# One weighted product of a two-layer graph kernel goes over to Strassen's scheme on pairs of row tiles

## The chip, the cores and the metric

The kernel runs on one NeuronCore of a Trainium2 chip. The metric is the device time of one execution in microseconds (us). Before the change it is 2158.61 us, the median of three runs (2158.42 to 2158.98).

The engines have the names of the profile: PE is TensorE (matmuls), PEld its loading of the stationary operand, DVE is VectorE, ACT is ScalarE, POOL is GpSimd, SP is SyncE, which mostly issues DMAs. Each engine has a queue of its own and works through it in order.

## The reference, cut to what matters

There are 3327 rows of 512 numbers (padded to 3328, that is 26 row tiles of 128), and an adjacency matrix of 3327 x 3327. Everything is float32.

```python
# layer 0
h = maximum(layernorm(x), 0)
q, k, v = h @ Wq.T + bq, h @ Wk.T + bk, h @ Wv.T + bv
a = q @ k.T / sqrt(512) + adj + adj
x = x + softmax(a) @ v
# layer 1
h = maximum(layernorm(x), 0)
A2 = adj + eye
d = diagonal(A2) ** -0.5
temp = A2 @ h @ W.T
x = x + relu((d[:, None] * A2 * d[None, :]) @ temp)
```

The kernel multiplies the unscaled exponentials P with h first and with Wv afterwards: `softmax(a) @ v` is `(P @ h @ Wv.T) / rowsum + bv`, because the rows of the softmax sum to one. So layer 0 ends, for each row tile, with a product of 128 x 512 by 512 x 512, a scaling by 1 / rowsum (`rs`), and the addition of `bv` and `x`. Layer 1 has a product of the same shape with W, scaled by `sd`, the d above.

## The kernel before, in words

**Scores.** 52 steps (four groups of columns, 13 pairs of row tiles) compute the scores. The function `fetch(k + 2)` loads the adjacency for two steps ahead on SP's queue. The queues of DVE, PE, POOL and SP are held to the order in which the code was written (`in_order`).

**The three large products.** Then come three products with a matrix of 3328 x 3328: g = 0 is P with h of layer 0, g = 1 is A2 with h of layer 1, g = 2 is A2 with `temp`. Each is cut by Strassen's scheme at the outside into seven parts (`ORDER`: p5, p1, p6, p7, p2, p3, p4), each part into two strips of columns (s = 0, 896 wide, and s = 1, 768 wide), each strip into seven steps: six with seven matmuls (t = 0 to 5) and an odd one with four (t = None). That makes 294 steps. The matmuls are 448 or 384 columns wide, half a strip. `Step.sums` makes three sums on DVE for each step, two steps ahead (`four_sums`, L164 to L166); `Right.make` makes the right sides (L171 to L174, L878 to L884); `Gather.first` (L962 to L966) and `Gather.rest` (L982) take the results of a strip out of PSUM at its end: `first` after the step t = 5, `rest` after the odd step. `Gather.seed` (L956, on ACT) puts a start value into the banks of the next strip.

**What is done beside the steps.** `run(k)` writes step k: its loads, its matmuls, with products of other work `inserted` between them, and then the DVE work that waits its turn in the list `waiting`. The dictionary `between` says what else belongs to step k; `number_of(g, r, s, t)` gives the number of a step. `post` puts a store off to the next step, on ACT's queue.

* Jobs: 52 sums (`Job`, L1017, 896 or 768 wide, on DVE) that layer 1 needs, one about every three steps from step 7 to step 164.
* The product with Wv: from step 79 (g = 0, p3, s = 1, t = 2) on, one row tile a step, 26 in all. `attend_load` loads x two steps ahead on ACT's queue; `attend` runs four matmuls of 512 columns into one PSUM bank after the step's matmuls (L1026), then on DVE the scaling with x added (L1038), `bv` added (L1039), and `norm` (L185 to L189 on DVE, L191 on POOL). `attended`, one step later, makes the row of h for layer 1 on ACT (L1045) and stores it. Wv and a copy of `bv` for all partitions are loaded at step 2 (`prepare`).
* The product with W (`Temp`): from step 177 on, one pair of row tiles for two steps. This one is already by Strassen's scheme: the 256 x 512 of the pair are four blocks of 128 x 256, and seven products of two 256-wide matmuls each stand for the eight block products. The two halves of one bank take the products in turn. After each product the bank's half is added into the result, which is called settling here: by ACT for p2, p5, p6 and p4 (L1091, a scaled write), by DVE for m1, p3 and p7 (L1093). Eight sums of 128 x 128 on DVE (L1077) make the left sides. The products stand at fixed places among the matmuls of steps k and k + 1, in this order:

```python
PARTS = (("p2", 1, True, 0, 1), ("m1", 0, True, 0, -1), ("p5", 1, False, 3, -1), ("p6", 0, False, 1, -1),
         ("p3", 1, False, 1, 1), ("p7", 0, False, 3, 1), ("p4", 0, False, 2, 1))
AFTER = ((0, 0), (0, 2), (0, 4), (0, 6), (1, 1), (1, 3), (1, 5))
```

The second column of `PARTS` is the half of the bank, the third says whether it starts anew, the fourth is the quarter of the result. `AFTER` says for each product the step (0 for k, 1 for k + 1) and after how many matmuls of it the product comes. The matmuls of a product that accumulates must wait until the settling before has read the same half.

## Time and profile before

The profiled execution took 2159.13 us; its span, which the views show, is 2157.3 us.

| | busy, us | share of the span |
|---|---|---|
| PE | 2137.5 | 99% |
| DVE | 1652.0 | 77% |
| PEld | 1180.9 | 55% |
| ACT | 273.1 | 13% |
| POOL | 68.1 | 3% |

| work on the profile's page | line | busy, us | mean of one, ns |
|---|---|---|---|
| matmuls of the product with Wv, 512 columns, from `ct` | L1026 | 61.6 | 592 |
| the same, from `part` | L1026 | 32.9 | 592 |
| matmuls of the product with W, 256 columns, from `rows` | L1087 | 53.5 | 380 |
| scaling and x (20 of the 26) | L1038 | 15.0 | 749 |
| adding `bv` (20 of the 26) | L1039 | 13.8 | 692 |
| first of a step's sums, 896 wide | L164 | 136.8 | 1086 |
| second and third, 448 wide, each | L165, L166 | 68.0, 68.1 | 624 |

A matmul in float32 leaves two records in the trace. A record's duration reaches past the start of the next record, since matmuls are pipelined; what one costs is read from the distance of two starts. The same holds on DVE to a smaller degree: when two instructions don't depend on one another, the second starts before the first has ended. A stretch's busy time counts such overlaps once.

### The profile page before, as it was taken

Reading aid. Unit: us, or ns where it says so; the run is one execution under the profiler, and the core shown is the slowest. Engines: PE = TensorE matmul, PEld = TensorE weight load, DVE = VectorE, ACT = ScalarE, POOL = GpSimd, SP = SyncE. Lnnn points to the kernel's source line nnn. Section 1 sums busy time; section 2 is a strip of 40 time slices with the busy share of each in tenths; the row PEclk is TensorE's granted clock in tenths of the full one; section 3 lists DMA queues with packets and bytes.
Section 4 is the critical chain, followed back from the end, with each engine's and each line's share of the span. In section 5 each row is a group of like instructions: output and inputs, shape, how many; then the busy total and the mean of one; then the engine's idle time right before and its main releaser. Section 6 shows DMA issues by size and latency. Waiting matters only on the chain.

```text
span 2157.3 us, 20906 instructions
## 1 busy us (share of the span) xinstructions
PE 2137.5 (99%) x6272; PEld 1180.9 (55%) x6272; DVE 1652.0 (77%) x3235; ACT 273.1 (13%) x441; POOL 68.1 (3%) x63
## 2 busy tenths in 40 slices
PE   9999999999999999999999999999999999999998
PEld 5555555555555555555454555555666665555554
DVE  7479888888887688776777778886566576778897
ACT  6311211112110000001111000010111100000000
POOL 2000000000004000000111000000000000000000
PEclk9999999999999999999999999999999999999999
DMA  8678888888999899889787889986646578978996
GB/s 305 210 257 303 296 311 282 306 289 291 337 308 299 292 370 330 278 296 309 267 308 260 303 283 368 321 303 221 203 146 201 150 225 252 303 229 247 261 293 167
DMA packets 402546, 592.10 MB, mean 274 GB/s; under 512 B 140012, under 2 KB 273528, under 8 KB 402424
## 3 DMA queue, kind: packets, MB, share of 16 engines
q1 hardware_dynamic: 374488, 533.12, 75.2%
q10 hardware_dynamic: 27936, 57.56, 7.3%
q8 instruction: 52, 0.85, 0.2%
q14 instruction: 70, 0.57, 0.1%
HBM read 422.71 MB, written 173.87 MB: 277 GB/s over the span
## 4 chain that ended last, share of the span: by engine, by line
PE 93%; DVE 4%; DMA 2%; issue 1%; POOL 0%; ACT 0%; SPq 0%; DVEq 0%
PE p L919 55%; PE Y L542 13%; PE Z L542 6%; PE p L910 5%; PE p L1026 4%; PE pw L1087 3%; PE X L542 3%; PE Y L398 2%; PE Z L398 1%; DMA rows<-row 1%; DMA part<-sum 1%; PE X L398 0%; DMA wk<-in_wk_dram 0%; DVE part L164 0%; DVE st L185 0%
## 5 line engine op out<-in xcount | busy, mean ns | idle before, releaser
L919 PE MATMUL p<-part,b 128*128 128x448 f32 (+1 forms) x3528 | 1257.6, 513 | 0.8 <-DVE part L165 0.6
L919 PEld LDWEIGHTS p<-part,b 128*128 128x128 f32 x3528 | 669.9, 190 | 542.1 <-issue 291.8
L542 PE MATMUL Y<-qt,hp 128*128 128x448 f32 (+1 forms) x832 | 308.2, 513 | 2.6 <-DVE g L546 1.8
L164 DVE TENSOR_TENSOR part<-part 128x896 f32<-128x896 f32 (+1 forms) x252 | 256.5, 1018 | 68.8 <-DMA part<-sum 29.6
L542 PEld LDWEIGHTS Y<-qt,hp 128*128 128x128 f32 x832 | 157.8, 190 | 136.3 <-issue 72.7
L542 PE MATMUL Z<-qt,hp 128*128 128x384 f32 (+1 forms) x416 | 162.3, 512 | 0.0
L166 DVE TENSOR_TENSOR part<-part,part 128x448 f32<-128x448 f32 (+1 forms) x219 | 129.4, 591 | 15.3 <-DVE part L165 0.5
L165 DVE TENSOR_TENSOR part<-part,part 128x448 f32<-128x448 f32 (+1 forms) x219 | 129.4, 591 | 7.2
L910 PE MATMUL p<-part,b 128*128 128x448 f32 (+1 forms) x336 | 124.2, 512 | 0.0
L542 PEld LDWEIGHTS Z<-qt,hp 128*128 128x128 f32 x416 | 79.0, 190 | 66.2 <-issue 37.9
L546 DVE SCALAR_TENSOR_TENSOR g<-g,Y 128x384 f32<-128x384 f32 (+1 forms) x156 | 91.3, 585 | 29.9 <-PE Y L542 28.4
L962 ACT COPY part<-p 128x384 f32<-128x384 f32 (+1 forms) x33 | 16.6, 503 | 656.1 <-PE p L919 497.8
L910 PEld LDWEIGHTS p<-part,b 128*128 128x128 f32 x336 | 63.8, 190 | 54.1 <-issue 31.0
L549 ACT ACTIVATE g<-g 128x768 f32<-128x768 f32 (+1 forms) x48 | 43.0, 896 | 347.5 <-DVE g L546 311.7
L542 PE MATMUL X<-qt,hp 128*128 128x384 f32 (+1 forms) x208 | 81.1, 512 | 0.0
L963 DVE TENSOR_TENSOR part<-p,part 128x384 f32<-128x384 f32 (+1 forms) x33 | 19.3, 585 | 62.2 <-PE p L919 61.4
L1026 PE MATMUL p<-w,ct 128*128 128x512 f32 x136 | 61.6, 592 | 0.0
L542 PEld LDWEIGHTS X<-qt,hp 128*128 128x128 f32 x208 | 39.5, 190 | 33.1 <-issue 19.3
L191 POOL TENSOR_TENSOR rstd<-ve,mhalf 128x1 f32<-128x1 f32 x46 | 38.4, 836 | 529.5 <-DVE ve L189 502.2
L982 DVE TENSOR_TENSOR ct<-p,part 128x448 f32<-128x448 f32 (+1 forms) x72 | 42.3, 608 | 16.2 <-PE p L910 12.1
L1087 PE MATMUL pw<-w,rows 128*128 128x256 f32 x208 | 53.5, 380 | 0.4 <-DVE rows L1077 0.4
L1017 DVE TENSOR_TENSOR job<-job 128x896 f32<-128x896 f32 (+1 forms) x52 | 52.9, 1017 | 0.0
(194 smaller groups left out, 1679.0 us busy)
## 6 DMA issues: line engine op xcount, KB each, us to landing
part<-sum SPq DMA_DIRECT2D x104, 448.0 KB, 5.3
part<-p SPq DMA_DIRECT2D x91, 448.0 KB, 6.0
part<-sum SPq DMA_DIRECT2D x104, 384.0 KB, 4.1
part<-p SPq DMA_DIRECT2D x91, 384.0 KB, 4.6
part<-in_adjT_dram SPq DMA_DIRECT2D x78, 448.0 KB, 5.1
b<-row SPq DMA_DIRECT2D x234, 128.0 KB, 4.9
part<-in_adjT_dram SPq DMA_DIRECT2D x78, 384.0 KB, 3.9
g<-in_adjT_dram SPq DMA_DIRECT2D x52, 448.0 KB, 4.2
```

The source lines that it names most:

```text
L164: yield nc.vector.tensor_add(o[:, 0:2], g[:, 0:4:3], g[:, 1:2].to_broadcast([P, 2, g.shape[-1]]))
L165: yield nc.vector.tensor_add(o[:, 2], o[:, 1], g[:, 0])
L166: yield nc.vector.tensor_add(o[:, 3], o[:, 2], g[:, 2])
L398: nc.tensor.matmul(ps[:, :w], M[B[name]][:, c, o * P : (o + 1) * P], hp[k][:, A[name], c], start=start and c == 0, stop=c == 1, skip_group ...
L542: nc.tensor.matmul(ps[:, :wd], h_of(self.t, name, k), qt[B[name]][:, k], start=start and k == 0, stop=k == 1, skip_group_check=True)
L546: nc.vector.scalar_tensor_tensor(a[n], a[n], 2.0, ps[:, :wd], op0=ALU.mult, op1=ALU.add if sign > 0 else ALU.subtract)
L549: nc.scalar.activation(g[1], g[1], AF.Exp, **({"bias": pad} if self.t == HALF - 1 else {}))
L910: yield nc.tensor.matmul(ps[("p2", "p3", "p4", "p8")[k]][:, :w], b[:, z], a[:, 0, y], start=k == 3 and not self.seeded, stop=True, skip_gr ...
L919: yield nc.tensor.matmul(ps[r][:, :w], b[:, i], m, start=self.t == 0 and not adds, stop=self.t == PAIRS - 1 and r in ("p1", "p5", "p6", "p ...
L1017: nc.vector.tensor_add(self.a, self.a, self.b)
L1026: nc.tensor.matmul(ps, cts[s][y][d][:, k * P : (k + 1) * P], w[d], start=d == 0, stop=d == DC - 1)
L1087: nc.tensor.matmul(ps, a, W[B[name]][:, c], start=new and c == 0, stop=c == 1, skip_group_check=True)
```

## The change

The product with Wv is now done by the same scheme as the product with W. `Attend` is a class derived from `Temp`, with the same seven products at the same places among the matmuls, starting at the same step 79, one pair for two steps. Its differences: `settled` is always one DVE instruction that multiplies the bank's half by 1 / rowsum or its negative (`rs`, `nrs`) and adds it to the tile of x in place; the left sides have other places in SBUF; after the last product both tiles are stored and normed, and `attended` makes the rows of h two and three steps after the pair began.

The blocks of Wv and their four differences are made like those of W (`load_weights`), from step 65 on. `bv` is no longer added on DVE. Instead, during the scores, `with_bias` writes x to a scratch tensor in DRAM tile by tile, with a copy on SP's queue in even steps, and adds `bv` to it with an accumulating DMA on POOL's queue in odd steps; `Attend.load` reads the scratch tensor where x was read before. The jobs are spread anew: 26 before step 72, one every five steps to step 107, then 18 from step 112 to 164, with other buffers in each stretch.

```diff
@@ -155,6 +155,7 @@
+    xbd = [dram.tile([P, D], F32, name=f"xb{i}") for i in range(NT)]
@@ -496,6 +497,15 @@
+    bv_rows = bass.AP(tensor=bv.tensor, offset=bv.offset, ap=[[0, P], [1, D]])
+
+    def with_bias(k):
+
+        if k % 2 == 0:
+            nc.sync.dma_start(xbd[k // 2], x[k // 2 * P : (k // 2 + 1) * P])
+        else:
+            nc.gpsimd.dma_start(xbd[k // 2], bv_rows, accum_op=ALU.add)
+
@@ -639,6 +649,7 @@
             fetch(k + 2)
+            with_bias(k)
@@ -711,24 +722,13 @@
...
     def prepare():
-        wv_w1.append(weights(wvT))
-        bvs.append(half(11, [P, D], "bv_sb"))
-        nc.sync.dma_start(bvs[0], bass.AP(tensor=bv.tensor, offset=bv.offset, ap=[[0, P], [1, D]]))
@@ -747,27 +747,36 @@
+        nc.scalar.mul(nrs, rs, -1.0)
+
+    W, V, differences = [], [], []
+
+    def load_weights(w, src, made):
+
+        w.extend(made)
+        for z in range(2):
+            for y in range(2):
+                block = src[z * E : (z + 1) * E, y * E : (y + 1) * E]
+                nc.sync.dma_start(w[2 * z + y], block.rearrange("(c p) e -> p c e", p=P))
+        differences.append(four_differences(w))
...
+    def value_weights():
+
+        b11, b21, b22, t1, t2, t3, t4, b12 = blocks((11, 12, 13, 14), "wv")
+        load_weights(V, wvT, (b11, b12, b21, b22, t1, t2, t3, t4))
+        attend_slots["h"] = b12.rearrange("p c e -> p (c e)")
@@ -808,10 +817,16 @@
-    job_ring = ring(*spare[2:], (half, 14))
...
+    job_rings = {n: ring(*of) for n, of in (("early", spare[1:]), ("amid", (spare[1], spare[4])), ("late", (*spare[2:], (half, 14))))}
...
@@ -1019,39 +1034,6 @@
-    def times_weights(i, w):
-        s, y, k = where(i)
-        ps = bank(ROLE["p8"], "p8")
-        for d in range(DC):
-            nc.tensor.matmul(ps, cts[s][y][d][:, k * P : (k + 1) * P], w[d], start=d == 0, stop=d == DC - 1)
-        return ps
...
-    def attend(i):
-
-        xt, ps = xts[i], times_weights(i, wv_w1[0])
-        nc.vector.scalar_tensor_tensor(xt, ps, rs[:, i : i + 1], xt, op0=ALU.mult, op1=ALU.add)
-        nc.vector.tensor_add(xt, xt, bvs[0])
-        post(x1_of(i), xt)
-        normed[i] = norm(xt)
...
@@ -1061,7 +1043,24 @@
...
+        def settled(self, name, to, ps, by):
+            if name in ("p2", "p5", "p6", "p4"):
+                nc.scalar.mul(to, ps, by)
+            else:
+                nc.vector.scalar_tensor_tensor(to, ps, by, to, op0=ALU.mult, op1=ALU.add)
...
@@ -1071,29 +1070,59 @@
...
+    class Attend(Temp):
+
+
+        def __init__(self, *its):
+            self.its, self.w, self.by, self.to = its, V, (rs, nrs), []
+
+        def load(self):
+            xt = next(attend_slots["x"])
+            nc.scalar.dma_start(xt, xbd[self.its[len(self.to)]])
+            self.to.append(xt)
...
+        def settled(self, name, to, ps, by):
+            nc.vector.scalar_tensor_tensor(to, ps, by, to, op0=ALU.mult, op1=ALU.add)
+
+        def end(self):
+            for i, xt in zip(self.its, self.to):
+                post(x1_of(i), xt)
+
+        def norms(self):
+            self.normed = []
+            for xt in self.to:
+                self.normed.append(norm(xt))
+                yield
+
+        def attended(self, n):
+            h1, (rstd, bias) = attend_slots["h"], self.normed[n]
+            nc.scalar.activation(h1, self.to[n], AF.Relu, bias=bias(), scale=rstd)
+            nc.scalar.dma_start(rowd[1][self.its[n]], h1)
@@ -1186,36 +1215,35 @@
-    jobs = [Job(k, s, j) for k in range(2) for s in range(2) for j in range(HALF)]
-    k0, k1 = number_of(0, 0, 1, 0), number_of(1, 5, 0, 0) - 4
-    for n, job in enumerate(jobs):
-        k = k0 + n * (k1 - k0) // len(jobs)
+    amid = number_of(0, 5, 1, 2) - 7
+    late, w1_at, k1 = number_of(1, 1, 0, 0), number_of(1, 4, 0, 0), number_of(1, 5, 0, 0) - 4
+    k0 = number_of(0, 0, 1, 0)
+    times = [k0 + n * (amid - k0) // 26 for n in range(26)] + [amid + 5 * n for n in range(8)]
+    times += [late + n * (k1 - late) // 18 for n in range(18)]
...
-    k = number_of(0, 5, 1, 2)
-    for i in ROW:
-        if steps[k].t is None:
-            k += 1
-        rows(k, i)
-        k += 1
...
+    def laid(k, make):
+
+        for n in range(0, NT, 2):
+            if steps[k].t is None:
+                k += 1
+            w = make(*ROW[n : n + 2])
+            sums_of[k] = w.sums
+            for j, (later, m) in enumerate(AFTER):
+                inserted.setdefault((k + later, m), []).append((w, j))
+            yield k, w
+            k += 2
+
+    for k, w in laid(number_of(0, 5, 1, 2), Attend):
+        for what, later, *args in ((w.load, -2), (w.load, -1), (w.norms, 1), (w.attended, 2, 0), (w.attended, 3, 1)):
+            at(k + later, what, *args)
```

## The prediction

> **What bounds the kernel now.** I read the page first (busy shares, then the chain that ended last), next TensorE's timeline where it computes the product with Wv and where it computes the other weighted product, then the busy time by stage, and last VectorE's timeline at the end of a strip.
>
> ```profile
> span 2157.3 us, 20906 instructions
> PE 2137.5 (99%) x6272; PEld 1180.9 (55%) x6272; DVE 1652.0 (77%) x3235; ACT 273.1 (13%) x441; POOL 68.1 (3%) x63
> PE 93%; DVE 4%; DMA 2%; issue 1%; POOL 0%; ACT 0%; SPq 0%; DVEq 0%
> ```
>
> TensorE is the bound nearly everywhere: fewer columns streamed is time gained, a TensorE wait is time lost. VectorE (DVE) is the next engine, at 77%.
>
> ```profile
> 1053.24 1.88 PE L1026 MATMUL p<-w,ct 128*128 128x512 f32 x4
> 1054.96 1.88 PE L1026 MATMUL p<-w,part 128*128 128x512 f32 x4
> 1056.68 5.42 PE L919 MATMUL p<-part,b 128*128 128x448 f32 x14
> ...
> 1597.87 1.03 PE L1087 MATMUL pw<-w,ct 128*128 128x256 f32 x4
> 1598.73 1.67 PE L919 MATMUL p<-part,b 128*128 128x448 f32 x4
> 1600.24 1.03 PE L1087 MATMUL pw<-w,rows 128*128 128x256 f32 x4
> ```
>
> Columns: start in us, length, work, xrecords. Each matmul leaves two records (passes). Starts give the price: eight 512-wide passes, one row tile, take 1056.68 - 1053.24 = 3.44 us (0.43 a pass); four 256-wide passes, one product of the Strassen class `Temp`, take 0.86 (0.215 a pass); two 448-wide matmuls take 1600.24 - 1598.73 = 1.50, 0.75 each. In the 384-wide strip a matmul takes 0.64 by the same ratio.
>
> ```profile
> 500.00:620.00 120.00, 118.25 (x366) 68.90 (x365) 106.23 (x224) 21.92 (x27) 0.00 (x0) 1.00 0.94 324
> 990.00:1216.00 226.00, 225.85 (x601) 113.85 (x600) 164.08 (x333) 26.85 (x38) 26.44 (x25) 1.00 0.84 288
> 1525.00:1750.00 225.00, 223.04 (x778) 146.86 (x777) 135.64 (x338) 30.59 (x65) 0.00 (x0) 1.00 0.58 180
> ```
>
> Columns: stretch, length, busy PE, PEld, DVE, ACT, POOL, clock, DMA share, GB/s. The second row is the stage that is changed: DVE busy 164 of 226, TensorE idle 0.15. The third is `Temp`'s stage, today's model of the new one: DVE 136 of 225, TensorE idle 1.96.
>
> ```profile
> 1558.19 0.55 DVE L963 TENSOR_TENSOR part<-p,part 128x384 f32<-128x384 f32 x1
> 1560.30 0.68 DVE L884 TENSOR_TENSOR b<-b,rows 128x512 f32<-128x512 f32 x1
> 1561.96 1.94 DVE L982 TENSOR_TENSOR part<-p,part 128x384 f32<-128x384 f32 x4
> 1563.96 0.45 ACT L1091 ACTIVATE ts<-pw,sd 128x256 f32<-128x256 f32 x1
> 1564.47 1.13 PE L1087 MATMUL pw<-w,ct 128*128 128x256 f32 x4 [1.37 <-ACT ts L1091]
> ...
> 1067.09 0.69 DVE L185 BATCH_NORM_STATS2 st<-part 128x6 f32<-128x512 f32 x1
> 1068.11 0.96 DVE L164 TENSOR_TENSOR part<-part 128x768 f32<-128x768 f32 x1
> 1070.17 0.62 DVE L963 TENSOR_TENSOR part<-p,part 128x448 f32<-128x448 f32 x1
> ```
>
> At a strip's end DVE works through a burst: four gather sums (1558.19 to 1560.30, 2.11 us), the five ops of a right side (1.66), four more gather sums (1.9). A norm takes 1067.09 to 1068.11, 1.02; a step's three sums 2.06 (384) and, by L164 to L166 in the 448 form, 2.32. And the fifth line: product m1 of a pair waits for the settling of p2, the product before it, though that one lies in the other half of the bank. There it waited 1.37 us, because ACT, which settles p2, was late.
>
> **The change, part by part.** *The product.* 13 pairs x 2 tiles x 3.44 = 89.4 us go; 13 x 7 x 0.86 = 78.3 come. **-11.2 us**, all of it on the path.
> Against half-wide matmuls speaks the Trainium skill, "TensorE: Matmul & The Clock Gate", section "Wait — 56ns, not 53.3ns?": a fixed 2.5 ns or so a matmul. With 156 passes more that would be an estimated 0.4 us of the gain; the starts above (0.43 against 2 x 0.215) show no such term.
>
> *DVE's load.* Per pair before: 2 x (0.78 + 0.73) = 3.0 us for L1038 and L1039, by starts. After: seven settlings and eight row sums, all on DVE. A 256-wide settling takes 482 ns (L1093), 0.40 start to start; a 128-wide add 0.20. 2.8 + 1.6 = 4.4. So 1.4 x 13 = 18 us more, 4 less for some four jobs that leave the stage: about 178 of 215 us, 83%. On average that is covered. In order it is not, and that is the next term.
>
> *Start of a strip.* Pairs begin at steps 84, 91, 98 and 105, each the first step of a strip, and m1 waits for p2's settling, now behind DVE's burst. In the changed kernel's order DVE has, between p4's settling of the pair before and p2's of this one (step 84): step sums 2.32, gather 2.11, right side 1.66, two norms 2.04 and their small op 0.07, gather 1.9, p2's settling 0.48: 10.6 us. Ahead of it stand 0.26 from TensorE's last pass to DVE's start and 0.40 for p4's settling; behind it 0.06 to TensorE: 11.3. In that time TensorE has two matmuls of 0.64, the odd step's four of 0.64, p2 (0.86) and two of 0.75: 6.2. It waits 5.0. Step 98 has the same list: 5.0. Step 91 has the widths exchanged and a job (1.0) for the right side: 10.9 against 6.7, 4.2. Step 105 has that without the job: 3.2. **+17.4 us.** Bounds: 1.4 each, the one such wait seen (5.6 in all), and the whole list uncovered by any overlap, 2 us more each (25). I take the worked sum: its terms are rows of the same burst.
>
> *Inside a pair.* p4 needs p7 settled, two matmuls earlier. In pair 0, between the settlings of p3 and p7 stand step sums 2.06 and a job 1.0: 0.26 + 0.40 + 3.06 + 0.48 + 0.06 = 4.3 from p3's end; TensorE arrives after 4 x 0.64 + 0.86 = 3.4. It waits 0.8. The same lists with norms, right sides or jobs between give waits in pairs 2, 3, 8 and 9 (0.2, 1.1, 0.2, 2.1). **+4.4**; bounds 0.6 (the 1.96 idle of `Temp`'s stage less 1.37) and 8.
>
> *The clock.* TensorE ends at 2147:
>
> ```profile
> 1562.00:1566.00 4.00, 2.63 (x9) 1.43 (x8) 3.49 (x8) 1.87 (x4) 0.00 (x0) 1.00 0.92 273
> 2148.00:2149.00 1.00, 0.00 (x0) 0.00 (x0) 0.38 (x2) 0.00 (x0) 0.00 (x0) 0.92 0.76 159
> 2149.00:2151.00 2.00, 0.00 (x0) 0.00 (x0) 0.00 (x0) 0.00 (x0) 0.00 (x0) 0.50 0.49 158
> ...
> L294 PE MATMUL idle<-zero x16: 421/421/582, 1.1 to 4.5; 128*128 128x128 f32 x16
> ```
>
> A gap of 1.37 us left it at 1.00; some 2 us after the last matmul it is at half. The kernel's first 16 passes of 128 columns took 3.4 us and more instead of 1.7 at the later pace: a drop costs about 1.9. Bounds: 0, and four drops, 7.6. The gaps of 3 to 5 us are nearer to the tail than to 1.37; three drops, less what DVE catches up meanwhile: **+4**.
> The skill's same page, "HAM oscillation — how this bites in real kernels", states the limit as idle gaps of about 3.4 us; by it three of the four gaps count, an estimate of the same size.
>
> *The bias in DRAM.* 26 copies on SP and 26 accumulating transfers on POOL's queue, during the scores (108 to 620). POOL does nothing else there; SP's copies wait for nothing and stand behind the step's loads. Bytes: 26 x 0.26 MB x 3 (copied, read, added) = 20 MB; at 324 / 0.94 = 345 GB/s 59 us of all 16 DMA engines in 515, a share of 0.11. Where the share is 0.80 to 0.88 it fits. In 500 to 620 it makes 1.05: up to 6 us late. Bounds 0 and 6; I take **+1**, since g is fetched two steps (20 us) ahead and lands in 4.2. No row shows an accumulating transfer.
>
> *At nothing.* Wv's four loads and its differences (4 x 0.7 on DVE, one op on ACT) move to steps 65 to 73, where DVE is 77% busy; without that cover they cost 2.8. 26 jobs come every 2.5 steps instead of 3: the same cover. `attended` comes one or two steps later; the first right sides of layer 1 are loaded at step 93 and want rows finished at 87 or 88 (row 10: 93 for 97), so h1 (4.4 us to land) stays ahead; if not, sums wait on a DMA as L164 does now. The first wait of the old stage (0.3) goes.
>
> Sum against the profiled run (2159.1; span 2157.3): -11.2 + 17.4 + 4.4 + 4 + 1 - 0.3 = +15.3, 2174.4. The median of the runs lies 0.5 lower: **2174**.
>
> **Rivals.** *Faster:* DVE reaches p2's settling in time. For it: `Temp` has the same order of products and the same bursts, and idles 1.96 us. Against: there ACT settles four of the seven, p2 and p4 among them, and no norm or job stands in DVE's queue. Price: 2159.1 - 11.2 + 2.0 - 0.3 = 2149.6, 2149 as median. It decides if the four waits are under 1.5 us each. *No change:* the waits come to about 11 us, without a drop of the clock: 2159. That needs DVE's list 2 us shorter at each strip and no waits inside pairs. *Slower still:* the accumulating transfers delay g or rows in the scores, 10 us or more on top: 2185 to 2195. For it: DMA share 0.94 in 500 to 620, where TensorE already idles 1.75. Against: from 200 to 500 TensorE is busy all of every stretch of 100 us, so the scores have had no late load there.
>
> **How the numbers follow.** Forecast 0.80, still slower 0.09, faster 0.07, no change 0.04. Low end: no drop of the clock, no DMA term, waits 8 us shorter: 2159.1 + 10.3 - 8 - 0.5 = 2161, and a little for the no-change case: 2160. High end: 7.6 for the clock and 6 for DMA, 2183, and part of the still slower case: 2190. Below 0.2% (4.3 us) a measurement here can't tell a change from none; the forecast lies wholly above it. Faster 0.07, same 0.05, slower 0.88.
>
> **What would show it.** Right: product records about 0.215 apart; in the stage of the new `Attend` four TensorE waits of 3 to 5 us on DVE's settling, at the strips' starts, clock below 1.00 after them; DVE near 83%. Wrong: no such waits, or ACT or DMA as their releaser; TensorE waiting in the scores. The forecast falls if DVE overlaps the burst with earlier steps more than the rows of before show.

## The result, and the profile after

The changed kernel takes 2222.26 us, the median of four runs (2220.06 to 2223.95), beside 2158.8 for the kernel before in the same session: a ratio of 1.0291, with an interval of 1.0273 to 1.0309. The forecast was 2174 with a range of 2160 to 2190. The direction was right and the size was not: of a loss of 63 us the prediction had accounted for 15.

The profiled execution of the kernel after took 2223.95 us, 64.8 more than the one before. Its page, with the span, the busy times and the shares of the chain of work that ended last:

```profile
span 2222.1 us, 21410 instructions
PE 2151.4 (97%) x6428; PEld 1214.9 (55%) x6428; DVE 1672.6 (75%) x3382; ACT 272.5 (12%) x443; POOL 76.9 (3%) x89
PE 76%; DMA 11%; DVE 10%; issue 2%; SPq 0%; ACT 0%; POOL 0%; ACTq 0%; DVEq 0%
```

In the chain, DMA has gone from 2% to 11% and DVE from 4% to 10%: there are two new costs, one of each kind. The windows tell their places (stretch, length, then busy PE, PEld, DVE, ACT and POOL, the clock, the DMA share, GB/s):

```profile
200.00:300.00 100.00, 94.91 (x262) 48.78 (x261) 76.83 (x151) 16.92 (x20) 4.07 (x5) 1.00 0.93 300
500.00:620.00 120.00, 109.43 (x320) 61.38 (x318) 90.90 (x186) 20.79 (x26) 4.88 (x6) 0.96 0.95 309
1030.00:1285.00 255.00, 235.53 (x792) 153.02 (x792) 189.67 (x487) 25.86 (x37) 14.32 (x26) 0.97 0.70 238
```

In the third row, the stage of `Attend`, TensorE idles 19 us, where it idled 0.15 before; this was foreseen. In the first two rows, the scores, it idles 5 in 100 and 11 in 120, where it was busy all of 200 to 300 and idled 1.75 in 500 to 620; this was not.

For all kernels below, one measure is worked out from the trace, stage by stage: the distances between the starts of TensorE's successive passes, less 0.838 ns per column streamed (0.215 us for 256 columns, 0.43 for 512). What is left is **lost time**: waits, and passes at a lower clock.

| lost time, us | prologue | scores | products of layer 0 | `Attend`'s stage | from there to `Temp` | `Temp` | rest | sum |
|---|---|---|---|---|---|---|---|---|
| before | 6.6 | 4.1 | 0.6 | 0.6 | 1.2 | 4.2 | 1.4 | 18.7 |
| after | 7.7 | 43.4 | 5.7 | 29.5 | 0.4 | 4.2 | 2.6 | 93.5 |

The sums differ by 74.8; less the 11.2 of streaming that the new scheme saves, 63.6 of the 64.8 are placed (the other 1.1 lie behind the last matmul). The new losses are 39.3 in the scores, 28.9 beside `Attend`, 5.1 in layer 0's products.

**Beside Attend.** TensorE's timeline where step 84 begins (start, length, work; in brackets the idle time before it and what ended it), then VectorE's timeline of the same moment:

```profile
1066.63 1.03 PE L1086 MATMUL pw<-wv,ct 128*128 128x256 f32 x4
1067.49 1.67 PE L934 MATMUL p<-part,b 128*128 128x448 f32 x4
1073.92 1.55 PE L1086 MATMUL pw<-wv,ct 128*128 128x256 f32 x4 [4.76 <-DVE xt L1110]
1075.26 2.98 PE L934 MATMUL p<-part,b 128*128 128x448 f32 x4
```

```profile
1062.96 0.48 DVE L1110 SCALAR_TENSOR_TENSOR xt<-pw,rs,xt 128x256 f32<-128x256 f32 x1 [1.40 <-PE pw L1086]
1063.36 1.08 DVE L165 TENSOR_TENSOR part<-part 128x896 f32<-128x896 f32 x1
...
1069.52 0.69 DVE L186 BATCH_NORM_STATS2 st<-part 128x6 f32<-128x512 f32 x1
...
1071.53 1.94 DVE L997 TENSOR_TENSOR part<-p,part 128x384 f32<-128x384 f32 x4
1073.39 0.47 DVE L1110 SCALAR_TENSOR_TENSOR xt<-pw,rs,xt 128x256 f32<-128x256 f32 x1
```

This is the list that the prediction wrote down: p4's settling at 1062.96, then sums, gather, right side, norms, gather, and at 1073.39 p2's settling, which frees m1 at 1073.92. The first product after the gap takes 1.55 where 1.03 is usual, and four 448-wide passes 2.98 instead of 1.67: the clock has dropped (granted 0.50 from 1075 to 1077 us).

**In the scores.** SP issues all loads and stores of the scores, in order. What it waited for, in 108 to 650 (us in total, times, longest), in the kernel before and then in the kernel after:

```profile
SPq L506 <- DMA p<-g: 126.1, 48, 6.1
SPq L534 <- DVE o L528: 55.0, 21, 16.7
```

```profile
SPq L516 <- DMA p<-g: 221.7, 48, 8.9
SPq L544 <- DVE o L538: 21.2, 4, 16.7
```

The load of `g` has to wait until the store of P out of the same buffer, of an earlier pair, has landed. Already in the kernel before, SP stood 126 us of the stage in that wait; after, 222. Two more answers of the kernel after, for the same stretch: its queues (packets, MB, share of the 16 engines), and what the loads did to DVE and TensorE.

```profile
q1 hardware_dynamic: 94542, 155.24, 81.4%
q0 software_dynamic: 3456, 6.29, 9.5%
```

```profile
DVE o L538 <- DMA g<-in_adjT_dram: 41.9, 23, 3.4
PE Y L552 <- DVE g L556: 25.5, 15, 8.4
DVE b L893 <- DMA rows<-row: 9.1, 1, 9.1
```

24 of POOL's 26 small transfers fall into this stretch. These 6 MB of 162 hold the engines for 9.5% of 542 us, that is 51 us. DVE then waits for `g`, and TensorE for DVE.

### The profile page after: what moved, and what is told of

Same layout as the page of the kernel before. It is cut to its first block, busy times and chain, and to the rows that moved or that the text cites. A ratio compares the mean times of both kernels' runs of the same rounds, so it can differ in the third digit from the quotient of the medians.

```text
span 2222.1 us, 21410 instructions
## 1 busy us (share of the span) xinstructions
PE 2151.4 (97%) x6428; PEld 1214.9 (55%) x6428; DVE 1672.6 (75%) x3382; ACT 272.5 (12%) x443; POOL 76.9 (3%) x89
## 4 chain that ended last, share of the span: by engine, by line
PE 76%; DMA 11%; DVE 10%; issue 2%; SPq 0%; ACT 0%; POOL 0%; ACTq 0%; DVEq 0%
PE p L934 51%; PE pw L1086 7%; PE Y L552 6%; PE p L925 4%; DMA p<-g 3%; DMA g<-in_adjT_dram 3%; PE Z L552 3%; PE Y L399 2%; PE X L552 1%; DVE g L556 1%; PE Z L399 1%; DVE part L165 1%; DMA sum<-o 1%; DMA rows<-row 1%; DVE o L538 1%
## 5 line engine op out<-in xcount | busy, mean ns | idle before, releaser
L934 PE MATMUL p<-part,b 128*128 128x448 f32 (+1 forms) x3528 | 1274.3, 514 | 2.3 <-DVE ct L997 1.9
L552 PE MATMUL Y<-qt,hp 128*128 128x448 f32 (+1 forms) x832 | 316.5, 523 | 25.7 <-DVE g L556 25.5
L167 DVE TENSOR_TENSOR part<-part,part 128x448 f32<-128x448 f32 (+1 forms) x219 | 129.4, 591 | 14.5
L925 PE MATMUL p<-part,b 128*128 128x448 f32 (+1 forms) x336 | 124.2, 512 | 0.0
L977 ACT COPY part<-p 128x384 f32<-128x384 f32 (+1 forms) x33 | 16.6, 502 | 626.2 <-PE p L934 468.3
L538 DVE TENSOR_TENSOR o<-g 128x384 f32<-128x384 f32 (+1 forms) x52 | 30.5, 587 | 37.7 <-DMA g<-in_adjT_dram 37.5
L552 PEld LDWEIGHTS X<-qt,hp 128*128 128x128 f32 x208 | 39.5, 190 | 33.1 <-issue 19.3
L997 DVE TENSOR_TENSOR ct<-p,part 128x448 f32<-128x448 f32 (+1 forms) x72 | 42.6, 609 | 15.7 <-PE p L925 11.2
L1086 PEld LDWEIGHTS pw<-w,rows 128*128 128x128 f32 x208 | 39.4, 190 | 19.8 <-issue 7.2
```

The source lines that it names most:

```text
L167: yield nc.vector.tensor_add(o[:, 3], o[:, 2], g[:, 2])
L538: nc.vector.tensor_add(o, *(g[k][:, y] for k, y in parts))
L552: nc.tensor.matmul(ps[:, :wd], h_of(self.t, name, k), qt[B[name]][:, k], start=start and k == 0, stop=k == 1, skip_group_check=True)
L925: yield nc.tensor.matmul(ps[("p2", "p3", "p4", "p8")[k]][:, :w], b[:, z], a[:, 0, y], start=k == 3 and not self.seeded, stop=True, skip_gr ...
L934: yield nc.tensor.matmul(ps[r][:, :w], b[:, i], m, start=self.t == 0 and not adds, stop=self.t == PAIRS - 1 and r in ("p1", "p5", "p6", "p ...
L1086: nc.tensor.matmul(ps, a, self.w[B[name]][:, c], start=new and c == 0, stop=c == 1, skip_group_check=True)
```

## The experiments

All fifteen kernels at a glance; lost time is the measure above, the ratio is to the kernel before on the same chip. Layer 0's products are "products", the stage between `Attend` and `Temp` is "later".

| kernel | scores | products | `Attend` | later | time, us | ratio (interval) |
|---|---|---|---|---|---|---|
| after | 43.4 | 5.7 | 29.5 | 0.4 | 2222.26 | 1.0291 (1.0273 to 1.0309) |
| e1, neither copies nor transfers | 3.9 | 5.6 | 29.2 | 1.1 | 2182.45 | 1.0112 (1.0095 to 1.0129) |
| e2, copies alone | 2.4 | 6.3 | 29.4 | 3.1 | 2184.34 | 1.0118 (1.0101 to 1.0135) |
| e3, before with both | 41.3 | 3.1 | 0.6 | 0.3 | 2197.14 | 1.0175 (1.0158 to 1.0192) |
| e4, plain on POOL, not paced | 2.7 | 6.2 | 30.6 | 0.4 | 2228.71 | 1.0325 (1.0307 to 1.0342) |
| e5, plain tile on POOL, paced | 10.5 | 7.2 | 29.4 | 1.9 | 2194.30 | 1.0156 (1.0137 to 1.0175) |
| e6, row of bv on SP | 13.9 | 17.8 | 30.6 | 2.2 | 2205.71 | 1.0203 (1.0185 to 1.0220) |
| e7, norms later | 3.8 | 5.8 | 19.9 | 0.5 | 2171.29 | 1.0050 (1.0030 to 1.0070) |
| e8, jobs spread | 4.1 | 1.3 | 31.1 | 15.0 | 2194.92 | 1.0152 (1.0134 to 1.0169) |
| e9, ACT settles | 2.0 | 5.9 | 26.4 | 5.9 | 2182.61 | 1.0106 (1.0089 to 1.0122) |
| e10, other rows added | 33.1 | 6.9 | 30.8 | 2.1 | 2214.43 | 1.0252 (1.0235 to 1.0270) |
| e11, row written plainly | 23.3 | 6.7 | 30.9 | 1.3 | 2202.51 | 1.0196 (1.0179 to 1.0213) |
| e12, added beside `Attend` | 1.7 | 15.9 | 31.5 | 1.6 | 2194.89 | 1.0169 (1.0152 to 1.0186) |
| e13, that and norms later | 3.3 | 15.0 | 22.8 | 0.3 | 2187.38 | 1.0139 (1.0122 to 1.0155) |
| e14, that and paced | 2.6 | 7.1 | 25.7 | 1.1 | 2181.07 | 1.0109 (1.0092 to 1.0126) |

Each row's losses are read from one profiled execution. The runs of one kernel lie up to 7.5 us apart (e6), so a difference of 2 or 3 us between two rows is not clear of noise.

### Where the 40 us of the scores come from: e1, e2, e3, e4

e1 takes the copies and transfers out of the kernel after (first diff), e2 the transfers alone (second), and e3 puts both into the kernel before, where nothing reads them (third).

```diff
-            with_bias(k)
...
-            nc.scalar.dma_start(xt, xbd[self.its[len(self.to)]])
+            i = self.its[len(self.to)]
+            nc.scalar.dma_start(xt, x[i * P : (i + 1) * P])
```

```diff
-        else:
-            nc.gpsimd.dma_start(xbd[k // 2], bv_rows, accum_op=ALU.add)
```

```diff
             fetch(k + 2)
+            with_bias(k)
```

> The changed kernel without the copies and the accumulating transfers during the scores; Attend reads x itself, so that the addition of bv is left out. Theory A (the DMAs of the scratch tensor delay the stores of P, these the buffers of g, and these the scores): TensorE's waits between 108 and 620 us fall from 42.7 to about 3.4, as before the change, those after them (5.3) mostly go too, and the time is 2222 - 39 - 5 - 1 = about 2177. What is left over the kernel before is the stage of Attend alone: -11.2 + 28.6 = +17. Rival R (the scores wait for something else that changed, such as the buffers of the jobs or Wv's later load): over 2200.

> The changed kernel with the copies of x to the scratch tensor on SP's queue, without the accumulating transfers; the addition of bv is left out. Theory A1 (the accumulating transfers cost the most: 6.8 MB in 2.5% of 16 engines over 2222 us is 55 us of all engines, the copies at the rate of the other transfers 21 us): 2177 plus a fourth of 40, 2187 at most. Rival A2 (the copies in SP's queue, ahead of the stores of P, are what delays them): over 2205, nearly the time of the changed kernel.

> The kernel before with the copies and the accumulating transfers added during the scores, and nothing else changed; the scratch tensor is read by nobody. Theory A: the price of the scratch tensor is the same without Attend, +40 to +45 us, 2200 to 2204, with waits of some 42 us between 108 and 620. Rival R: under 2175.

e1 takes 2182.45, e2 2184.34, e3 2197.14. Without copies and transfers the scores lose 3.9 us, as before the change; with the copies alone 2.4; with both added to the kernel before, and nothing else, 41.3. So the loss in the scores comes with the 26 transfers on POOL's queue; the copies, 6.8 MB on SP's queue, cost nothing by themselves. No run has the transfers without the copies. Two times were missed by a little: in e1 (2177 expected) the 5.6 us in the products were to go with the transfers and stayed, which e8 takes up, and e3 is 3 us under its band.

e4 makes the transfer a plain one, into a second scratch tensor that nobody reads.

```diff
-            nc.gpsimd.dma_start(xbd[k // 2], bv_rows, accum_op=ALU.add)
+            nc.gpsimd.dma_start(xbe[k // 2], bv_rows)
```

> The changed kernel with bv written by a plain transfer on POOL's queue into a second scratch tensor, instead of the accumulating one; the copies stay, the addition of bv is left out. Theory A1 in the form that adding is what is slow (each byte read twice and written): POOL's transfers cost about the copies' 21 us of engine time, the time is 2190 to 2197. Rival A3 (POOL's queue is slow whatever the transfer does): as the changed kernel, 2215 or more.

The time is 2228.71, no lower than that of the kernel after, but not for the reason asked about. A plain transfer into a tensor of its own has nothing to wait for, and POOL does nothing else: all 26 went out between 1.3 and 67.4 us, in the prologue, which then lost 50.9 us instead of 7.7, while the scores lost 2.7. Whether adding, the row of bv or POOL's queue is the price could not be read from that.

### What in a transfer costs: e5, e6, e10, e11

In four kernels the transfers keep the pace of the scores, the addition of `bv` is left out, and the transfer itself is changed. In place of the accumulating transfer, e5 copies, on POOL, the tile that SP's copy has just written:

```diff
-            nc.gpsimd.dma_start(xbd[k // 2], bv_rows, accum_op=ALU.add)
+            nc.gpsimd.dma_start(xbe[k // 2], xbd[k // 2])
```

e6 writes the row of bv from SP's queue:

```diff
+            nc.sync.dma_start(xbe[k // 2], bv_rows)
```

e10 adds 128 different rows of x in place of one row 128 times:

```diff
+            nc.gpsimd.dma_start(xbd[k // 2], x.rearrange("(p i) d -> i p d", i=NT)[k // 2], accum_op=ALU.add)
```

and e11 writes the row of bv plainly over the copy:

```diff
+            nc.gpsimd.dma_start(xbd[k // 2], bv_rows)
```

> The kernel after, but the transfer on POOL's queue is a plain one: it copies a tile of the scratch, which SP's copy has just written, into a second scratch tensor, which Attend reads. It has to wait for SP's copy, so the 26 transfers keep the pace of the scores, as in the kernel after. No row of bv is read and nothing is added (the addition of bv is left out). Theory Q, a transfer on POOL's queue costs what it costs, whatever it carries: waits of TensorE in the scores 35 to 46 us, time 2215 to 2228. Theory A, the adding, or the 2 KB row of bv that is read 128 times, is what slows the engines: scores under 15 us, time 2184 to 2196. In both the stage of Attend keeps its 29 us of waits.

> The kernel after, but the transfer of the row of bv goes out on SP's queue, plainly, into a second scratch tensor that nothing reads; POOL's queue carries nothing in the scores (the addition of bv is left out). The bytes read and written are those of the plain transfer on POOL, and the source is the same row, read 128 times. Theory Q: as good as the copies alone, scores 2 to 6 us, time 2182 to 2187. Theory A in its form that reading one row 128 times is the cost: scores 25 us and more, time 2205 and above.

> The kernel after, but POOL's accumulating transfer adds 128 different rows of x, 26 apart, of 2 KB each, where the kernel after adds the one row of bv 128 times; Attend reads x and nothing reads the scratch (the addition of bv is left out). Theory A1, adding is what holds the engines: as in the kernel after, 35 to 44 us of waits in the scores, time 2214 to 2226. Theory A2, one row read 128 times is what holds them: like a plain transfer on POOL's queue, 7 to 15 us, time 2187 to 2197.

> The kernel after, but POOL's transfer writes the row of bv plainly over the copy, with nothing added; it has to follow SP's copy and so keeps the pace of the kernel after. Attend reads x and nothing reads the scratch (the addition of bv is left out). Theory A1: like the plain transfer of a tile on POOL's queue, 7 to 15 us of waits in the scores, time 2187 to 2197. Theory A2: as in the kernel after, 35 to 44 us, time 2214 to 2226. If each of the two carries part, both this run and the one that adds other rows lie between, 20 to 30 us.

No single theory held. e5 (10.5 us in the scores) rules out that any transfer on POOL's queue costs 40. e10 (33.1) and e11 (23.3) both lie between the ends: adding and reading the one row each carry a part. What orders the kernels with transfers on POOL's queue is how long these hold the engines. Time of q0 in 108 to 650 (its share of the 16 engines times 542 us) beside the lost time of the scores:

| | q0's share | of 16 engines, us | lost in the scores, us |
|---|---|---|---|
| e5, plain, tile | 3.2% | 17 | 10.5 |
| e11, plain, row | 5.0% | 27 | 23.3 |
| e10, added, other rows | 7.7% | 42 | 33.1 |
| after, added, row | 9.5% | 51 | 43.4 |

From the first row to the last, 34 us more of the engines cost 33 us more of TensorE: about one to one from end to end, and less evenly between neighbours (10 us for 13, 15 for 10, 9 for 10). Yet the copies' bytes cost nothing. The windows of the whole stage, of the kernel before, of e2, of the kernel after and of e6, suggest why, though the last does not fit (columns as above):

```profile
108.00:650.00 542.00, 539.38 (x1540) 291.80 (x1539) 458.35 (x887) 101.48 (x121) 0.00 (x0) 1.00 0.87 296
```

```profile
108.00:650.00 542.00, 541.17 (x1545) 292.70 (x1544) 460.26 (x889) 101.65 (x121) 0.00 (x0) 1.00 0.90 306
```

```profile
108.00:650.00 542.00, 512.05 (x1431) 272.57 (x1429) 422.48 (x818) 95.12 (x112) 19.54 (x24) 0.98 0.91 299
```

```profile
108.00:650.00 542.00, 531.93 (x1511) 285.45 (x1509) 444.32 (x856) 99.84 (x117) 0.00 (x0) 1.00 0.89 313
```

The DMA share was 0.87 before, is 0.90 with the copies, and 0.91 or 0.92 in e5, e10, e11 and after, whatever POOL's queue adds. Read as a ceiling of this stage, that leaves some 22 us to give away from 0.87 to 0.91; the copies take most of them, and what comes on top is paid in full. SP's wait for the store of P grows in the same order: 126 (before), 167 (e2), 182 (e5), 204 (e11), 214 (e10), 222 (after). That this wait, a store's round trip in which SP can issue nothing, is what keeps the stage's share under 0.92 is argued from these rows; no run removed it.

e6 shows that SP's own queue pays as well: it adds as many bytes as e5 and loses 13.9 in the scores, and another 12 in the products, where the work left over from the scores holds DVE up (the longest wait there, 7.9 us, is for the small `tiled` tile at 662, behind a queue of sums). Theory Q expected it to be free, and its "not POOL, no cost" falls: the second 6.8 MB cost, the first did not. But the ceiling doesn't explain e6. Its share is 0.89, below that of e2, and SP's wait for the store of P is 181 us, no longer than in e5. SP has 26 more transfers to issue there, in order between the loads and stores; whether its queue is then the limit was not tested.

### Whether the price is of the stage or of the transfer: e12, e13, e14

e12 issues the same accumulating transfers four and five steps ahead of their pair. Most of them then run beside `Attend`, whose DMA share in e1 is 0.71. e13 has the later norms and the order of products of e7 (below) besides.

```diff
-        else:
-            nc.gpsimd.dma_start(xbd[k // 2], bv_rows, accum_op=ALU.add)
...
+        def bias_load(self, n):
+            nc.gpsimd.dma_start(xbd[self.its[n]], bv_rows, accum_op=ALU.add)
...
-        for what, later, *args in ((w.load, -2), (w.load, -1), (w.norms, 1), (w.attended, 2, 0), (w.attended, 3, 1)):
+        for what, later, *args in ((w.bias_load, -5, 0), (w.bias_load, -4, 1), (w.load, -2), (w.load, -1), (w.norms, 1), (w.attended, 2, 0), (w.attended, 3, 1)):
```

> The whole computation. The copies stay in the scores; the 26 accumulating transfers, unchanged in form and number, are issued four and five steps ahead of their pair, so that all but some five of them run beside Attend, where the DMA engines are busy 0.69 of the time, instead of beside the scores, where they are busy 0.91. Theory C, the scores have a ceiling of DMA work at about 0.91 (their share was 0.87 before and stood at 0.90 to 0.92 in every variant) and what lies above it is paid one to one: moved to where there is room, the transfers cost 0 to 5 us: scores 2 to 5, products 5 to 9, Attend's stage 29 to 32, time 2182 to 2190. Theory T, an accumulating transfer holds up whatever runs beside it: the 40 us come back in the products and Attend's stage, time 2205 and above.

> The whole computation: the transfers issued ahead of their pair, as in the run beside this one, and the norms of a pair one step later with two of its products one place earlier, as in the run in which that shortened the four waits. If the two causes are separate, their gains add: Attend's stage 20 to 23 us, time 2171 to 2180, still above the kernel before by the waits that are left there and by the jobs' 5 us. If the transfers beside Attend make VectorE's burst or the x tiles later, the stage goes above 26 and the time above 2183.

The 19 transfers beside `Attend` cost about 2 us (31.5 for 29.4), and the scores lose 1.7. So the transfer is not dear by itself; it was dear where it stood. The time is 2194.89 all the same, above the band of theory C, because the products lose 15.9 instead of 6. e13 misses its band for the same reason: 2187.38, with 15.0 in the products, while `Attend`'s stage has the 22.8 that were expected. POOL's queue in 620 to 985 of e12 (packets, MB, share of the 16 engines), and its issues there (count, KB, median us to land):

```profile
q0 software_dynamic: 1008, 1.84, 4.0%
```

```profile
xb<-in_bv_dram POOLq DMA_DIRECT2D x7, 256.0 KB, 17.0
```

Seven transfers went out between 689.6 and 693.0 us, 17 us to land each, though they are written at steps 74 to 81, some 280 us later. POOL's queue holds nothing ahead of them that would keep them back to their place, as in e4. e14 is e13 with the first eight made to wait: their copies, which the transfers need, are issued nine and eight steps ahead of the pair instead of in the scores.

```diff
-        if k % 2 == 0:
+        if k % 2 == 0 and k // 2 not in ROW[:8]:
...
+        def copy_load(self, n):
+            i = self.its[n]
+            if i in ROW[:8]:
+                nc.sync.dma_start(xbd[i], x[i * P : (i + 1) * P])
...
-        for what, later, *args in ((w.bias_load, -5, 0), (w.bias_load, -4, 1), (w.load, -2), (w.load, -1), (w.norms, 2), (w.attended, 3, 0), (w.attended, 4, 1)):
+        for what, later, *args in ((w.copy_load, -9, 0), (w.copy_load, -8, 1), (w.bias_load, -5, 0), (w.bias_load, -4, 1), (w.load, -2), (w.load, -1), (w.norms, 2), (w.attended, 3, 0), (w.attended, 4, 1)):
```

> The whole computation, as in the run with transfers beside Attend and norms later, but the copies of the first eight tiles are issued nine and eight steps ahead of their pair instead of in the scores. POOL's transfers wait for these copies, so the first eight can't go out in one burst at 690 us, in the middle of the products, but go out one at a time from about 940. Theory C, a transfer costs what the DMA engines have no room for at that moment: the products' waits fall from 15 to 5 to 9 us, the rest stays (scores 2 to 5, Attend 20 to 25), time 2174 to 2181. Rival, the waits at 720 and 760 have another cause than the burst, the copies before it or the order of the jobs: products still 13 to 16, time 2183 and above.

The first eight now go out from 956.0 to 1002.7, one or two at a time, and the products lose 7.1 instead of 15.0; `Attend`'s stage takes 3 us back (25.7 for 22.8), with its DMA share at 0.89. With 2181.07 (the expected band ended at 2181) this is, with e9 below (2182.61), the best version here of the whole computation by the new scheme, 41 us under the kernel after and 22 above the kernel before; the intervals of the two overlap.

### The waits at the starts of strips: e7, e9

e7 starts from e1 and takes the two norms out of DVE's burst.

```diff
-        for what, later, *args in ((w.load, -2), (w.load, -1), (w.norms, 1), (w.attended, 2, 0), (w.attended, 3, 1)):
+        for what, later, *args in ((w.load, -2), (w.load, -1), (w.norms, 2), (w.attended, 3, 0), (w.attended, 4, 1)):
...
-            for j, (later, m) in enumerate(AFTER):
+            for j, (later, m) in enumerate(((0, 0), (0, 2), (0, 4), (0, 6), (1, 0), (1, 2), (1, 5)) if make is Attend else AFTER):
```

> The kernel after without its copies and accumulating transfers (Attend reads x, the addition of bv is left out), and with the two norms of a pair taken one step later, so that they leave VectorE's burst at the start of a strip; the first two products of a pair's second step come one place earlier. Theory: m1 waits for p2's settling behind VectorE's queue, so taking 2.1 us of norms from the burst shortens each of the four waits by about 1.2 to 1.9 us (4.92, 4.11, 4.92, 3.10 become about 3.6, 2.4, 3.7, 1.4) and TensorE's clock drops at two gaps instead of three: the stage's waits go from 29 to 19 to 22 us, time 2173 to 2177. Rival, the wait is for something other than VectorE's queue (a DMA, the bank): waits unchanged, 2182.

The four waits go from 4.92, 4.11, 4.92 and 3.10 to 3.13, 2.10, 3.19 and 1.10: each is shorter by 1.7 to 2.0 us, about the length of the two norms. (The two products that move are p3 and p7; p4, p2 and m1, between which the list of DVE's work runs, keep their places.) The stage loses 19.9 instead of 29.2, and the time is 2171.29, a little under what was expected. So the waits are for DVE's queue.

e9 does the whole computation with ACT settling p2, p5, p6 and p4 as in `Temp`, and POOL adding `bv` and x in SBUF.

```diff
-        def settled(self, name, to, ps, by):
-            nc.vector.scalar_tensor_tensor(to, ps, by, to, op0=ALU.mult, op1=ALU.add)
...
+            for xt in self.xs:
+                nc.gpsimd.tensor_add(xt, xt, attend_slots["h"])
+            for i, ts, xt in zip(self.its, self.to, self.xs):
+                nc.gpsimd.tensor_add(ts, ts, xt)
+                post(x1_of(i), ts)
```

> The whole computation of the kernel after, with two things done otherwise. ScalarE settles p2, p5, p6 and p4, as in Temp, into a fresh pair of tiles; x is loaded a step later, POOL adds bv to it in SBUF and adds it to the settled tile; the norms follow one step later, both rows are attended together two steps later, and there are no copies or transfers for bv in the scores. Theory: the four waits at the starts of strips are waits for VectorE's queue, so with p2 settled by ScalarE they go, and TensorE's waits in the stage fall from 29 us to 8 to 14; the scores keep 4, the products their 5; time 2161 to 2168. Rival: POOL's adds (four of 1.2 to 1.9 us a pair) or ScalarE, which also seeds at a strip's start, become what m1 or the norms wait for: 20 us and more in the stage, time 2173 and above.

2182.61: the rival was right. The stage still loses 26.4, and three of the four waits remain (5.27, 1.84, 2.80). At 1028 p2's settling on ACT stands behind the seeds of the next strip (L977), and these wait for DVE's last gather sums (L1003). ACT's timeline there, and below it POOL's and then DVE's at the same place of a later strip:

```profile
1031.40 1.48 ACT L977 ACTIVATE p<-ct 128x448 f32<-128x448 f32 x3 [8.01 <-DVE part L1003]
1032.82 0.45 ACT L1063 ACTIVATE xt<-pw,rs 128x256 f32<-128x256 f32 x1
```

```profile
1140.10 3.02 POOL L1117 TENSOR_TENSOR xt<-xt,wv 128x512 f32<-128x512 f32 x2
1143.08 1.27 POOL L1119 TENSOR_TENSOR part<-part,xt 128x512 f32<-128x512 f32 x1
1144.31 1.71 POOL L1119 TENSOR_TENSOR xt<-xt 128x512 f32<-128x512 f32 x1
```

```profile
1139.75 0.62 DVE L166 TENSOR_TENSOR part<-part,part 128x448 f32<-128x448 f32 x1
1140.41 1.57 DVE L167 TENSOR_TENSOR part<-part,part 128x448 f32<-128x448 f32 x1
1141.91 0.54 DVE L984 TENSOR_TENSOR part<-p,part 128x384 f32<-128x384 f32 x1
...
1144.93 1.23 DVE L172 TENSOR_TENSOR b<-b 128x128 f32<-128x128 f32 x1
```

So DVE's burst still ends the wait, through ACT. And the burst is longer: while POOL adds, L167 takes 1.57 us instead of 0.62 and L172 1.23 instead of 0.29. The gather sum L984, which reads one operand from PSUM, keeps its 0.54. The Trainium skill ("SBUF — State Buffer", section "Who interferes with whom") says that a VectorE instruction with both inputs in SBUF contends with a GpSimd instruction that reads SBUF; these rows agree.

### The jobs: e8

e8 is e1 with 21 jobs ahead of the stage instead of 26, and 23 instead of 18 behind it.

```diff
-    times = [k0 + n * (amid - k0) // 26 for n in range(26)] + [amid + 5 * n for n in range(8)]
-    times += [late + n * (k1 - late) // 18 for n in range(18)]
+    times = [k0 + n * (amid - k0) // 21 for n in range(21)] + [amid + 5 * n for n in range(8)]
+    times += [late + n * (k1 - late) // 23 for n in range(23)]
```

> The kernel after without its copies and accumulating transfers (Attend reads x, the addition of bv is left out), with the jobs set back towards the spread of before: 21 of them ahead of Attend's stage, every 3 steps, instead of 26 every 2.5, and 23 instead of 18 behind it. Theory: the denser jobs bring the 5 us of waits in layer 0's products (three waits of 1.2, 1.6 and 1.8 us for late step sums): these fall to about 1 to 2 us, time 2178, with up to 3 us coming back behind the stage, where the jobs stand denser. Rival, these waits belong to the loads of Wv or to the place of each job and not to their number: still 4 to 6 us, time 2182 to 2185.

The first half held: the products lose 1.3 instead of 5.6. The second did not: 15.0 are lost behind the stage, where e1 loses 1.1 and up to 3 more were expected, with step sums that wait for loads (21.2 us in 1300 to 1400, up to 6.9 at once). The time is 2194.92. Neither spread of the jobs is free.

What the three waits of e1's products (1.2, 1.6 and 1.8 us, at 753, 779 and 821) have in common stands in DVE's timeline. Ahead of each, a step's first sum has waited for its load:

```profile
745.93 1.09 DVE L165 TENSOR_TENSOR part<-part 128x896 f32<-128x896 f32 x1 [6.82 <-DMA part<-p]
...
779.24 1.09 DVE L165 TENSOR_TENSOR part<-part 128x896 f32<-128x896 f32 x1 [2.96 <-DMA part<-p]
...
814.96 1.09 DVE L165 TENSOR_TENSOR part<-part 128x896 f32<-128x896 f32 x1 [4.19 <-DMA part<-p]
```

## Why the prediction was right, and where it failed

What the prediction said of `Attend`'s stage held; its term for the scores did not.

**The product, -11.2.** Right within 0.5 us, with one reading of it wrong. Averaged over all passes that follow the one before without a wait, the distances of the kernel before are 109.1, 215.8, 322.5, 375.8 and 429.2 ns for 128, 256, 384, 448 and 512 columns: 0.833 a column and about 2.5 ns a pass. So the fixed term, of which the prediction said that the starts show none, is there; 0.43 and 0.215 were too coarse to show it. With 156 passes more, the scheme saves 10.7 us (208 x 429.2 less 364 x 215.8).

**Start of a strip, +17.4.** Right, wait by wait: 5.0, 4.2, 5.0 and 3.2 were predicted, 4.92, 4.11, 4.92 and 3.10 measured, 17.1 in all. (The first sum, 11.3 less 6.2, is 5.1 and not 5.0.) e7 shows the mechanism. The sign "DVE near 83%" was not seen: DVE is busy 182 us, for 178 predicted, but the stage is longer by its waits, 244 us, which makes 75%.

**Inside a pair, +4.4.** Right pair by pair: 0.8, 0.2, 1.1, 0.2 and 2.1 were predicted for pairs 0, 2, 3, 8 and 9, and 0.7, 0.2, 1.0, 0.2 and 2.1 measured, 4.2 us.

**The clock, +4.** A little low, within its bounds: twenty passes at half speed cost 5.6 us, and two in which the clock changed 0.3. They follow the gaps of 4.9, 4.1 and 4.9; after the 3.1 us gap at 1246 the clock stayed at 1.00. So three of four gaps counted, as forecast, though not by their length alone: in e7 the clock dropped after gaps of 3.1 and 3.2 us, so that the count came out is in part luck. These three terms are 27 of the 28.9 us that the stage lost; the rest is mostly some 0.1 us in the first pass after each wait.

**The bias in DRAM, +1, bounds 0 and 6.** This is the step that failed: it was about 40, nearly two thirds of the whole change. The load was not the error. 59 us of all engines were charged, and measured are some 20 for the copies, if their 6.8 MB go at the 345 GB/s of the prediction, and 51 for the transfers. The error was what the stage could take. "Where the share is 0.80 to 0.88 it fits" took every idle microsecond of the engines as free, 67 or so in 515, while the stage's share went no higher than 0.92 in any run, which leaves some 22. And "g is fetched two steps (20 us) ahead" reads the place in the code, not the queue: SP issues the load of g only when a store of P has landed, and the row of SP's waits, 126 us, already showed it. TensorE "busy all of every stretch" from 200 to 500 was read as slack, but showed only that no load had yet come too late. The same facts stood in the rival "still slower", which was given 0.09 and 10 us or more; its mechanism (late `g`) was the right one and its 2185 to 2195 too low.

**At nothing.** The 26 jobs every 2.5 steps were not covered: 5.1 us in the products, by e8. The argument was DVE's cover, and it left out the loads: each of the three waits in e1 stands behind a step sum that had waited 3.0 to 6.8 us for `part<-p`. In 625 to 985 DVE stands 30.9 us in such waits in e1, 22.6 in the kernel before and 23.0 in e8. A late load alone does not decide, since one of 5.9 us in e8 (at 747) costs TensorE nothing; and that the DMA engines had no room left is not shown: their share in 700 to 840 is 0.94 in e1 and 0.93 in the kernel before. The loads and differences of Wv, and the later rows, cost nothing that shows.

**Against the rivals.** "Faster" assumed that DVE would reach p2's settling in time; it didn't, and e9 shows that `Temp`'s way out does not carry over, since POOL's adds lengthen the burst. "No change" needed 11 us of waits; there were 29 beside `Attend` alone.

**Left open.** Why one row read 128 times costs more than 128 rows (e11 and e5 differ in the size of their packets too, 4 KB and 16 KB, and after and e10 only in the row: 51 against 42 us of the engines); what keeps the stage's share at 0.92 or less; and what makes e6 slow below it. No version here beats the kernel before: e7, the fastest, leaves out the addition of bv and is still 11 us slower.

## What to carry to other kernels

An idle share of the DMA engines isn't room: ask first which queue issues the loads that matter and what it waits for; in a stage where that queue already stands in a store's round trip, as here, count the time that a new transfer holds the engines, above the little that is free, at full price until a run shows less. A transfer costs what its stage can't take, so move it to where the engines idle, and give it something to wait for, since POOL's queue, with nothing to wait for, sent its transfers out long before their place in the code. On the compute side, a list of the instructions between two dependent ones, with their durations from the trace, gave each of the four waits here to about a tenth of a microsecond.

## What the hardware showed that had not been expected

* A 256 KB transfer between two places in DRAM on POOL's queue holds the 16 engines for 0.7 us (plain, 16 KB packets: 17 us in 25 transfers) to 2.1 us (added, one row: 51 in 24). The Trainium skill ("DMA: Bandwidth & Descriptors", section "Issuing engines are not separate DMA queues") says that the DMAs of all issuing engines run on the same 16 DMA engines; the 448 KB loads of `g` agree, which took 5.2 us to land beside the added transfers and 4.2 without them (e2).
* POOL issued 26 transfers within 67 us of the start (e4), and seven within 3.4 us (e12), hundreds of microseconds ahead of the code around them.
* The clock dropped after a gap of 2.0 us in the products of the kernel after (at 795), and not after one of 3.1 us (at 1246). The Trainium skill ("TensorE: Matmul & The Clock Gate", section "HAM oscillation — how this bites in real kernels") has a limit of about 3.4 us of idle time; here the length of the gap alone did not decide.
* Sums of VectorE with both inputs in SBUF took up to 1.57 us instead of 0.62 beside POOL's adds (e9).
* A matmul pass cost 0.833 ns a column and about 2.5 ns more, whatever its width (128 to 512 columns, kernel before).
